# A counting sort whose one-hots and counts change their layout, and a feed-forward cut to the real nodes

## The chip, the cores and the metric

The kernel runs on one core of one Trainium2 chip, as one launch. The metric is the device time in microseconds (us). The median of the runs shown is 3781.26 us.

The engines are called as the profile calls them: PE is TensorE (PEld its weight loads), DVE is VectorE, ACT is ScalarE, POOL is GpSimd, and SP is SyncE, which issues most DMAs. Each takes its instructions in program order.

## What is computed

A graph block with three parts, over 3125 nodes of 256 features:

```python
xn = _layernorm(x)
x = x + gnn(xn, edge_attr_64, src, dst, ...)   # 103125 edges: messages, segment_sum by dst, a small MLP
      + mix(xn, ...)                           # 4 layers: linear attention with 8 heads, feed-forward 256-1024-256
x = x + moe(_layernorm(x), edge_index, ...)    # 65536 edges: graph attention gives gates, 4 experts, top 2
```

In the third part the graph attention takes its softmax and its sums over the edges that end in one node (cut to what matters):

```python
e = leaky_relu(a_src[src] + a_dst[dst])
e_max = segment_max(e, dst)
ee = exp(e - e_max[dst])
denom = segment_sum(ee, dst)
agg = segment_sum(h[src] * (ee / denom[dst])[:, :, None], dst)
```

The edges come in any order. The kernel sorts the 65536 by dst first, so that the segments become runs.

## The kernel before, in words

Nodes lie in 25 tiles of 128 rows (the last has 53 real ones), and in chunks of four tiles (seven chunks, the last with one tile).

*The order of the work.* The main program walks through the four layers of the mixing part: keys, context, attend, feed-forward up (`ff_up`, which puts a gelu of 8 blocks of 128 features into `gT`) and feed-forward down (`ff_down`). Two other streams are woven in by hand. `pace` counts estimated microseconds and emits DVE's running sums of messages (`sum_up`, tile `m_run`, L490), after each eight of which POOL gathers eight more columns (L478); once those are through, it emits POOL's sends of sorted edges (`send`, L770). `beside` emits jobs of the sort from a list: 64 count groups, `starts`, some node jobs, then 64 place groups. A scheduler then orders each engine's instructions. After the mixing part come the graph attention over the sorted edges and the four experts, with L1211, L1301 and L1312.

*The sort.* A destination has a high digit (dst // 32, 128 bins) and a low digit (dst % 32). The edges are taken 128 x 8 at a time: `GC` = 8 columns make a group, and 64 groups cover them.

- `count_group` builds a one-hot of the high digit (`oh_hi`, 128 x 8) and of the low digit (`oh_lo`, 32 x 8) on DVE (L668). Both have the column index innermost. Eight matmuls (L683) with `oh_hi[:, :, i]` stationary and `oh_lo[:, :, i]` moving give the 128 x 32 counts of each column in PSUM. ACT casts them (L685) into the f16 tile `counts`, laid as 32 low digits by 9, with slot 0 of each nine kept at zero. A DMA writes it to `counts_d`, and a matmul with the identity (L690) adds it into `table`.
- `starts` sums the table into the start of every bin.
- `place_group` reads the group's counts back as `run` (`parts`, L699) and writes into slot 0 of each nine what `split` leaves of the start after rounding (L695). DVE scans along each nine (L728), which gives running counts. ACT makes `earlier` (L741) from PE's products of the transposed high one-hot `ohT` (L740). One group later PE forms `look`: for each column a sum of matmuls with `all_h` (L746), `near`, `run` and `earlier` (L753). Each has `ohT` or `earlier` stationary, and `near`, `run[:, :, i]` or `oh_lo[:, :, i]` moving. DVE picks each edge's own entry (`own_bin`, L755) and sums it up (L756); that is the edge's place.

`near` is one contiguous row of 32 f16. `run[:, :, i]` steps by 9 elements, 18 bytes, and `oh_lo[:, :, i]` by 8 elements, 16 bytes.

*Buffers.* `run` and `oh_lo` have three buffers, `oh_hi` two, `counts` two, the PSUM tile `ps_g` two.

Of the kernel before, what the change touches and what calls it, by code (L numbers as in the profile page):

```python
# [8 lines left out]
F32 = mybir.dt.float32  # L9
BF16 = mybir.dt.bfloat16  # L10
I32 = mybir.dt.int32
F16 = mybir.dt.float16
AF = mybir.ActivationFunctionType
ALU = mybir.AluOpType
AX = mybir.AxisListType
# [3 lines left out]
P = 128  # L19
N = 3125  # L20
NT = 25
# [18 lines left out]
E2 = 65536  # L40
TE = E2 // P
NEXP = 4
GC = 8
GROUPS = TE // GC
SRC = 4096
LO = 32
# [12 lines left out]
def kernel(ctx: ExitStack, tc: tile.TileContext, a: dict, out: bass.AP):  # L59
    nc = tc.nc  # L60
    ctx.enter_context(nc.allow_non_contiguous_dma(reason="short vectors by partition"))
    V, S, G, T = nc.vector, nc.scalar, nc.gpsimd, nc.tensor

    const = ctx.enter_context(tc.tile_pool(name="const", bufs=1))
# [3 lines left out]
    pg = ctx.enter_context(tc.tile_pool(name="pg", bufs=2, space=PSUM))  # L68
    pa = ctx.enter_context(tc.tile_pool(name="pa", bufs=3, space=PSUM))
    pt = ctx.enter_context(tc.tile_pool(name="pt", bufs=2, space=PSUM))  # L70
    px = ctx.enter_context(tc.tile_pool(name="px", bufs=1, space=PSUM))
# [9 lines left out]
                    base=0, channel_multiplier=-1)  # L81
    after = const.tile([P, P], F32, name="after")
    G.affine_select(out=after, in_=ones, pattern=[[-1, P]], compare_op=ALU.is_gt, fill=0.0,
                    base=0, channel_multiplier=1)
# [13 lines left out]
    ids = const.tile([P, P], F32, name="ids")  # L98
# [81 lines left out]
    so = ctx.enter_context(tc.tile_pool(name="so", bufs=1))  # L180
# [41 lines left out]
    ps = pg.tile([P, DM], F32, name="ps_g")  # L222
# [106 lines left out]
    lo = so.tile([P, TE], F16, name="lo")  # L329
    hi = so.tile([P, TE], F16, name="hi")  # L330
# [8 lines left out]
    ps = pt.tile([P, 512], F32, name="ps_t")  # L339
# [12 lines left out]
    G.iota(bins, pattern=[[1, P], [0, GC]], base=0, channel_multiplier=0, allow_small_or_imprecise_dtypes=True)  # L352
    bin_p = const.tile([P, 1], F32, name="bin_p")
    G.iota(bin_p, pattern=[[0, 1]], base=0, channel_multiplier=1, allow_small_or_imprecise_dtypes=True)
    ident_h = const.tile([P, P], F16, name="ident_h")
    V.tensor_copy(ident_h, ident)
    all_h = const.tile([P, P], F16, name="all_h")
# [14 lines left out]
    goes = const.tile([P, LO, GC + 1], F16, name="goes")  # L372
# [9 lines left out]
    def etile(name, dt=F32, shape=(P, NT)):  # L382
        return mi.tile(list(shape), dt, name=name)

    node_n, prev_t, whole_t, above = (etile(n) for n in ("node_n", "prev_t", "whole_t", "above"))
    cnt2n = etile("cnt2n", shape=(P, 2, NT))
    sums_ps = px.tile([P, LO * GC + 2 * NT], F32, name="sums_ps")

    table, whole_ps, first_ps = sums_ps[:, :LO * GC], sums_ps[:, LO * GC:LO * GC + NT], sums_ps[:, LO * GC + NT:]

    def ends_begin():
        offs = etile("offs")
# [23 lines left out]
    cnt, own_n = etile("cnt_n"), etile("own_n")  # L416
# [249 lines left out]
    def one_hot(t, dig, n, name, bufs):  # L666
        o = so.tile([P, n, GC], F16, name=name, bufs=bufs)
        V.tensor_tensor(o, bins[:, :n, :], dig[:, t:t + GC].rearrange("p (o t) -> p o t", o=1).to_broadcast([P, n, GC]),  # L668
                        op=ALU.is_equal)
        return o  # L670

    counts_d = dram.tile([GROUPS, P, LO * (GC + 1)], F16, name="counts_d")
    counted = []
    cnts = [so.tile([P, LO, GC + 1], F16, name=f"counts{k}") for k in range(2)]
# [2 lines left out]

    def count_group(t):
        if t < TE:
            ohh, ohl = one_hot(t, hi, P, "oh_hi", 2), one_hot(t, lo, LO, "oh_lo", 3)  # L680
            ps = pg.tile([P, LO, GC], F32, name="ps_g")
            for i in range(GC):
                T.matmul(ps[:, :, i], ohh[:, :, i], ohl[:, :, i], start=i == 0, stop=i == GC - 1, skip_group_check=True)  # L683
            cnt = cnts[t // GC % 2]
            S.copy(cnt[:, :, 1:], ps)  # L685
            nc.sync.dma_start(counts_d[t // GC, :, :], cnt.rearrange("p l i -> p (l i)"))
            counted.append((t, cnt))
        if t:
            t, cnt = counted.pop(0)
            T.matmul(table, ident_h, cnt[:, :, 1:], start=t == 0, stop=t + GC == TE, skip_group_check=True)  # L690

    def split(x, near, rest):

# [1 line left out]
        V.tensor_tensor(rest[:, :, 0], x, near, op=ALU.subtract)  # L695

    def parts(t):
        cnt = so.tile([P, LO, GC + 1], F16, name="run", bufs=3)
        nc.sync.dma_start(cnt.rearrange("p l i -> p (l i)"), counts_d[t // GC, :, :])  # L699
        return (so.tile([P, LO], F16, name="near", bufs=3), cnt)  # L700

    def starts():
        cnt2 = so.tile([P, LO], F32, name="cnt2", tag="base")
        V.tensor_reduce(cnt2, table.rearrange("p (l i) -> p l i", i=GC), AX.X, ALU.add)
        cum2 = so.tile([P, LO], F32, name="cum2", tag="oh_lo", bufs=3)
        V.tensor_tensor_scan(cum2, ones[:, :LO], cnt2, 0.0, op0=ALU.mult, op1=ALU.add)
        ps = pg.tile([P, LO], F32, name="ps_g")
        T.matmul(ps[:, :1], before, cum2[:, LO - 1:], start=True, stop=True)
        V.tensor_tensor(cum2, cum2, cnt2, op=ALU.subtract)
        base2 = so.tile([P, 1], F32, name="base2")  # L710
        V.tensor_copy(base2, ps[:, :1])
        V.tensor_scalar(cum2, cum2, base2, None, op0=ALU.add)
        nc.sync.dma_start(start_d, cum2)
        V.tensor_scalar(cum2, cum2, half, None, op0=ALU.add)
        places.append(parts(0))
        split(cum2, *places[0])

    def place_group(t):

        late = looks.pop() if looks else None  # L720
        if t < TE:
            hr = so.tile([P, GC, P], F16, name="hr", bufs=2)
            nc.sync.dma_start(hr.rearrange("p t e -> p (t e)"), row_h[t // GC:t // GC + 1, :].to_broadcast([P, P * GC]))
            ohT = ohTs[t // GC % 2]
            V.tensor_scalar(ohT[:P - 1], hr[:P - 1], bin_p[:P - 1], 2.0, op0=ALU.is_equal, op1=ALU.mult)
            ohl = one_hot(t, lo, LO, "oh_lo", 3)
            near, run = places.pop()
            V.tensor_tensor_scan(run.rearrange("p l i -> p (l i)"), goes.rearrange("p l i -> p (l i)"),  # L728
                                 run.rearrange("p l i -> p (l i)"), 0.0, op0=ALU.mult, op1=ALU.add)
            if t + GC < TE:  # L730
                base = so.tile([P, LO], F32, name="base")
                V.tensor_tensor(base, run[:, :, GC], near, op=ALU.add)
                places.append(parts(t + GC))
                split(base, *places[0])

            earlier = so.tile([P, GC, P], F16, name="earlier", bufs=2)
            for i0 in range(0, GC, 4):
                ps = pt.tile([P, 4, P], F32, name="ps_t")
                for i in range(4):
                    T.matmul(ps[:, i, :], ohT[:, i0 + i, :], ohT[:, i0 + i, :], start=i == 0, stop=i == 3, skip_group_check=True)  # L740
                S.activation(earlier[:, i0:i0 + 4, :], ps, AF.Sign, bias=slope[:, 2:3], scale=slope[:, 1:2])  # L741
            looks.append((t, ohT, ohl, near, run, earlier))
        if late:
            t, ohT, ohl, near, run, earlier = late
            look = pg.tile([P, GC, LO], F32, name="ps_g")
            T.matmul(look.rearrange("p i l -> p l i"), all_h, ohl, start=True, stop=False, skip_group_check=True)  # L746
            for k in range(3):
                for i in range(GC):
                    if k == 2:
                        a1, a2 = earlier[:, i, :], ohl[:, :, i]  # L750
                    else:
                        a1, a2 = ohT[:P - 1, i, :], run[:P - 1, :, i] if k else near[:P - 1]
                    T.matmul(look[:, i, :], a1, a2, start=False, stop=k == 2, skip_group_check=True)  # L753
            own = so.tile([P, GC, LO], F32, name="own_bin", bufs=1)
            V.scalar_tensor_tensor(own, look, float(E2), ohl.rearrange("p l i -> p i l"), op0=ALU.add, op1=ALU.mult)  # L755
            V.tensor_reduce(number[t // SG % 2][:, t % SG:t % SG + GC], own, AX.X, ALU.add)  # L756
            if (t + GC) % SG == 0:
                V.tensor_scalar_mul(number[t // SG % 2], number[t // SG % 2], 0.5)
                laid(place[:, t + GC - SG:t + GC], number[t // SG % 2])
                clock["placed"] = t + GC  # L760

    places = []
# [331 lines left out]
            pace(1.9 * k / 2)  # L1094

    def ff_up(l, c, h2, f0, f1):
        w = len(c) * P
        for f in range(f0, f1):
            ps = pa.tile([P, 512], F32, name="ps_a")
            for kc in range(2):  # L1100
                T.matmul(ps[:, :w], ff_w[l]["w1"][:, kc, f * P:(f + 1) * P], h2[:, kc, :w], start=kc == 0, stop=kc == 1)  # L1101
            S.activation(gT[:, f, :w], ps[:, :w], AF.Gelu, bias=ff_w[l]["b1"][:, f:f + 1])  # L1102
            pace(1.8 * len(c) / 4)
# [267 lines left out]
    goes, whole, whole_r, ends_in = (at_end[:, i:i + 1] for i in range(2 * H4 + NCH + 2, 2 * H4 + NCH + 6))  # L1371
# [31 lines left out]
    for t0 in (0, NT // 2 + 1):  # L1403
        t1 = min(t0 + NT // 2 + 1, NT)
        ps = pa.tile([P, NT // 2 + 1, NCA], F32, name="ps_a")
# [14 lines left out]
    own = node(H4, "own")  # L1420
# [94 lines left out]
    for j, c in enumerate(PAIRS):  # L1515
        if c[0] % HALF == 0:
            gates(c[0], min(c[0] + HALF, NT))
        for i, t in enumerate(c):
            if j % 3 == 2:

                for e0 in range(0, NEXP, 2):
                    w = so.tile([P, 2, D], F32, name="weighed", tag="hr", bufs=2)
# [38 lines left out]
```

## Time and profile before

| | |
|---|---|
| median of 3 timed runs | 3781.26 us (3776.46 to 3784.04) |
| the profiled execution's own time | 3726.91 us |
| its span, first to last instruction | 3725.2 us |
| mean granted clock of TensorE | 0.762 |
| busy: PE, PEld, DVE, ACT, POOL | 2232.7, 1505.7, 1452.2, 1062.2, 1776.0 us |
| first to last column gathered (L478) | some 17 to 1640 us |
| count groups (oh_hi at L668) | mostly 201 to 435 us |
| place groups (scans at L728) | 439 to 2700 us |

A line of a group gives the source line, the engine, the operation, output and inputs by the program's names, the shape and the number; then the busy time in us and the mean ns of one, then the engine's idle time just before them and what ended it. Durations of one instruction overlap with the next one's, so on PE the distance from start to start is what an instruction takes from the engine. "remote" is a wait whose end the trace ties to no instruction; "issue" is time without a visible wait.

### The profile page before, as it was taken

The numbers are of one execution on the slowest core, as the hardware profiler recorded it, in microseconds if no ns is written. First come the engines' busy times: TensorE is split into PE (matmuls) and PEld (weight loads), VectorE is DVE, ScalarE is ACT, GpSimd is POOL, SyncE is SP. The second block draws the span as 40 slices with busy tenths as digits, with TensorE's granted clock in tenths as the row PEclk, the third lists the DMA queues.
The fourth block names the chain that finished last, engine by engine and source line by source line (L and its number), as shares of the span: only waits on it lengthen the run. The fifth ranks groups of instructions, "written<-read, shape, count | busy, mean of one in ns | idle before, by whom it ended". The sixth has DMA issues, their size and how long they took to land. (4 is left out here: it accounts for less than half of the span.)

```text
span 3725.2 us, 31745 instructions
## 1 busy us (share of the span) xinstructions
PE 2232.7 (60%) x9891; PEld 1505.7 (40%) x9891; DVE 1452.2 (39%) x4484; ACT 1062.2 (29%) x1933; POOL 1776.0 (48%) x1843
## 2 busy tenths in 40 slices
PE   3667654675667676645575466547667275747470
PEld 2545433443444455433343344435445143424250
DVE  6656544644544455532232233324422021111127
ACT  4422242233233233322232224213333021212122
POOL 2545454544445544644435434453442736464623
PEclk8878776776778887877787777768788677868685
DMA  6656564746645556722010002101100101010101
GB/s 206 193 188 201 162 199 136 211 157 192 212 150 190 176 166 209 225 80 77 20 33 18 23 18 58 43 25 35 44 10 8 16 17 30 15 29 14 27 12 36
DMA packets 300669, 359.57 MB, mean 97 GB/s; under 512 B 180576, under 2 KB 248039, under 8 KB 287687
## 3 DMA queue, kind: packets, MB, share of 16 engines
q1 hardware_dynamic: 229782, 242.00, 20.4%
q0 software_dynamic: 70704, 115.42, 11.9%
q8 instruction: 80, 1.31, 0.1%
q14 instruction: 103, 0.84, 0.1%
HBM read 201.91 MB, written 155.35 MB: 96 GB/s over the span
## 5 line engine op out<-in xcount | busy, mean ns | idle before, releaser
L478 POOL DMA_INDIRECT m_run<-xn_d,src_i x806 | 797.5, 989 | 835.9 <-issue 228.2
L770 POOL DMA_INDIRECT by_dst<-pairs,place x512 | 494.8, 966 | 280.3 <-issue 185.5
L1211 POOL DMA_INDIRECT rows_c<-tab_d,si x400 | 380.6, 952 | 301.5 <-DVE rows_c L1269 182.6
L1101 PE MATMUL ps_a<-h,w 128*128 128x512 f32 (+1 forms) x896 | 413.0, 604 | 101.5 <-ACT gT L1102 38.5
L490 DVE SCALAR_TENSOR_TENSOR m_run<-m_run,stay 128x320 f32<-128x320 f32 x805 | 437.3, 543 | 32.3 <-DMA m_run<-xn_d,src_i 17.7
L1112 PE MATMUL ps_a<-w,gT 128*128 128x256 f32 x1600 | 382.3, 394 | 20.4 <-issue 19.9
L1112 PEld LDWEIGHTS ps_a<-w,gT 128*128 128x128 f32 x1600 | 314.4, 198 | 124.2 <-issue 78.4
L1301 PE MATMUL ps_a<-hT,we 128*128 128x512 f32 (+1 forms) x448 | 226.5, 640 | 137.9 <-issue 115.1
L1101 PEld LDWEIGHTS ps_a<-h,w 128*128 128x128 f32 x896 | 173.8, 214 | 267.5 <-issue 189.5
L1312 PE MATMUL ps_t<-we,hf 128*128 128x256 f32 x800 | 203.7, 406 | 111.6 <-issue 79.1
L609 PE MATMUL ps_a<-gh,gw 128*128 128x256 f32 (+1 forms) x312 | 106.4, 489 | 207.7 <-DVE gh L612 95.8
L1312 PEld LDWEIGHTS ps_t<-we,hf 128*128 128x128 f32 x800 | 160.2, 204 | 158.5 <-issue 97.9
L1301 PEld LDWEIGHTS ps_a<-hT,we 128*128 128x128 f32 x448 | 89.7, 213 | 294.0 <-issue 259.2
L1102 ACT ACTIVATE gT<-ps_a,b 128x512 f32<-128x512 f32 (+1 forms) x224 | 141.3, 641 | 214.3 <-PE ps_a L1101 118.8
L1261 DVE COPY rows_c<-ev 128x104 f32<-128x104 f32 (+1 forms) x16 | 4.6, 286 | 481.7 <-ACT ev L1223 471.3
L559 POOL DMA_INDIRECT aggr<-run_d,sum_i x25 | 24.4, 977 | 336.2 <-PE ps_t L585 312.9
L609 PEld LDWEIGHTS ps_a<-gh,gw 128*128 128x128 f32 x312 | 72.7, 250 | 235.9 <-DVE gh L612 102.2
L741 ACT ACTIVATE earlier<-ps_t,slope 128x512 f16<-128x512 f32 x128 | 93.8, 773 | 260.0 <-PE ps_t L740 146.2
L1039 PE MATMUL ps_g<-xm,kr 128*128 128x256 f32 x400 | 127.5, 463 | 63.8 <-ACT kr L1037 36.1
L123 ACT ACTIVATE hn<-xm,rstd 128x256 f32<-128x256 f32 x225 | 121.4, 592 | 86.5 <-DVE rstd L119 57.7
L1039 PEld LDWEIGHTS ps_g<-xm,kr 128*128 128x128 f32 x400 | 88.4, 232 | 118.3 <-ACT kr L1037 58.5
L159 PE MATMUL ps_t<-ident,hn 128*128 128x128 f32 x450 | 82.7, 319 | 87.6 <-issue 37.7
(399 smaller groups left out, 3615.6 us busy)
## 6 DMA issues: line engine op xcount, KB each, us to landing
run_d<-m_run SPq DMA_DIRECT2D x100, 1280.0 KB
m_run<-in_edge_attr_dram SPq DMA_DIRECT2D x95, 256.0 KB
hr<-row_h SPq DMA_DIRECT2D x64, 256.0 KB
m_run<-xn_d,src_i POOLq DMA_INDIRECT x806
w<-in_L_mix_W_dram SPq DMA_DIRECT2D x8, 1024.0 KB
by_dst<-pairs,place POOLq DMA_INDIRECT x512
rows_c<-tab_d,si POOLq DMA_INDIRECT x400
run_d<-rows_c SPq DMA_DIRECT2D x15, 312.0 KB
```

The source lines that it names most:

```text
L123: S.activation(dst, src, AF.Identity, bias=r[:, 1, i:i + 1], scale=r[:, 0, i:i + 1])
L478: last_gather[0] = G.indirect_dma_start(out=m[:, t, :D], out_offset=None, in_=xn_d, in_offset=bass.IndirectOffsetOnAxis(ap=src_i[:, t0 + t ...
L490: add = V.scalar_tensor_tensor(m[:, t, :], before_m, stay[:, c:c + 1], m[:, t, :], op0=ALU.mult, op1=ALU.add)
L609: T.matmul(ps[:, :w], gw[i][:, kc, m * P:(m + 1) * P], h[:, kc, :w], start=kc == 0, stop=kc == 1)
L770: i = G.indirect_dma_start(out=by_dst, out_offset=bass.IndirectOffsetOnAxis(ap=place[:, t:t + 1], axis=0), in_=pairs0[:, t:t + 1], in_offs ...
L1039: T.matmul(ps_x[:, m, :], kr[:, m * P:(m + 1) * P], xm[:, t, :], start=i == 0 and m == 0, stop=i == len(c) - 1, skip_group_check=True)
L1101: T.matmul(ps[:, :w], ff_w[l]["w1"][:, kc, f * P:(f + 1) * P], h2[:, kc, :w], start=kc == 0, stop=kc == 1)
L1102: S.activation(gT[:, f, :w], ps[:, :w], AF.Gelu, bias=ff_w[l]["b1"][:, f:f + 1])
L1112: T.matmul(ps[:, i, :], gT[:, f, (2 * i0 + i) * P:(2 * i0 + i + 1) * P], ff_w[l]["w2"][:, f, :], start=False, stop=f == FF // P - 1, skip_ ...
L1211: G.indirect_dma_start(out=rows_c[:, t - COLS[j], :], out_offset=None, in_=tab_d, in_offset=bass.IndirectOffsetOnAxis(ap=si[:, t:t + 1], a ...
L1301: T.matmul(ps[:, :w], we1[:, kc, f * P:(f + 1) * P], hT[:, kc, c[0] * P:c[0] * P + w], start=kc == 0, stop=kc == 1)
L1312: T.matmul(ps[:, i, :], hh[f][:, (i0 + i) * P:(i0 + i + 1) * P], we2[:, f, :], start=False, stop=f == FF2 // P - 1, skip_group_check=True)
```

## The change

The low one-hot gets the column index outside and the low digit inside (`low_hots`), compared with a new f16 ramp `low_ids`. The counts in PSUM have the same layout, and ACT's cast turns them back to 32 by 9 while it writes. The matmul into the table takes all nine slots, zeros included, and the table is 288 wide. After the scan a new ACT copy `run_c` turns the eight running counts of each digit into a contiguous row for each column; it takes the buffers of `counts`, and `run` has two buffers in place of three. `ff_up` takes only the 53 real nodes of the last chunk.

```diff
+    low_ids = const.tile([P, LO], F16, name="low_ids")
+    V.tensor_copy(low_ids, ids[:, :LO])
...
+    TW = LO * (GC + 1)
+    sums_ps = px.tile([P, TW + 2 * NT], F32, name="sums_ps")
...
+    def low_hots(t):
+        o = so.tile([P, GC, LO], F16, name="oh_lo", bufs=3)
+        V.tensor_tensor(o, low_ids.rearrange("p (o l) -> p o l", o=1).to_broadcast([P, GC, LO]),
+                        lo[:, t:t + GC].rearrange("p (t o) -> p t o", o=1).to_broadcast([P, GC, LO]), op=ALU.is_equal)
+        return o
...
-            ohh, ohl = one_hot(t, hi, P, "oh_hi", 2), one_hot(t, lo, LO, "oh_lo", 3)
-            ps = pg.tile([P, LO, GC], F32, name="ps_g")
+            ohh, ohl = one_hot(t, hi, P, "oh_hi", 2), low_hots(t)
+            ps = pg.tile([P, GC, LO], F32, name="ps_g")
             for i in range(GC):
-                T.matmul(ps[:, :, i], ohh[:, :, i], ohl[:, :, i], start=i == 0, stop=i == GC - 1, skip_group_check=True)
+                T.matmul(ps[:, i, :], ohh[:, :, i], ohl[:, i, :], start=i == 0, stop=i == GC - 1, skip_group_check=True)
             cnt = cnts[t // GC % 2]
-            S.copy(cnt[:, :, 1:], ps)
+            S.copy(cnt[:, :, 1:].rearrange("p l i -> p i l"), ps)
...
-            T.matmul(table, ident_h, cnt[:, :, 1:], start=t == 0, stop=t + GC == TE, skip_group_check=True)
+            T.matmul(table, ident_h, cnt.rearrange("p l i -> p (l i)"), start=t == 0, stop=t + GC == TE, skip_group_check=True)
...
-        cnt = so.tile([P, LO, GC + 1], F16, name="run", bufs=3)
+        cnt = so.tile([P, LO, GC + 1], F16, name="run", bufs=2)
...
-            ohl = one_hot(t, lo, LO, "oh_lo", 3)
-            near, run = places.pop()
-            V.tensor_tensor_scan(run.rearrange("p l i -> p (l i)"), goes.rearrange("p l i -> p (l i)"),
-                                 run.rearrange("p l i -> p (l i)"), 0.0, op0=ALU.mult, op1=ALU.add)
+            ohl = low_hots(t)
+            near, run_l = places.pop()
+            V.tensor_tensor_scan(run_l.rearrange("p l i -> p (l i)"), goes.rearrange("p l i -> p (l i)"),
+                                 run_l.rearrange("p l i -> p (l i)"), 0.0, op0=ALU.mult, op1=ALU.add)
+            run = so.tile([P, GC, LO], F16, name="run_c", tag=f"counts{t // GC % 2}")
+            S.copy(run, run_l[:, :, :GC].rearrange("p l i -> p i l"))
...
-            T.matmul(look.rearrange("p i l -> p l i"), all_h, ohl, start=True, stop=False, skip_group_check=True)
+            T.matmul(look, all_h, ohl, start=True, stop=False, skip_group_check=True)
...
-                        a1, a2 = earlier[:, i, :], ohl[:, :, i]
+                        a1, a2 = earlier[:, i, :], ohl[:, i, :]
...
-                        a1, a2 = ohT[:P - 1, i, :], run[:P - 1, :, i] if k else near[:P - 1]
+                        a1, a2 = ohT[:P - 1, i, :], run[:P - 1, i, :] if k else near[:P - 1]
...
-            V.scalar_tensor_tensor(own, look, float(E2), ohl.rearrange("p l i -> p i l"), op0=ALU.add, op1=ALU.mult)
+            V.scalar_tensor_tensor(own, look, float(E2), ohl, op0=ALU.add, op1=ALU.mult)
...
     def ff_up(l, c, h2, f0, f1):
-        w = len(c) * P
+        w = min((c[-1] + 1) * P, N) - c[0] * P
```

More of the change, by code (lines that the diff above doesn't have):

```diff
@@ L386 @@
     cnt2n = etile("cnt2n", shape=(P, 2, NT))
-    sums_ps = px.tile([P, LO * GC + 2 * NT], F32, name="sums_ps")
-    table, whole_ps, first_ps = sums_ps[:, :LO * GC], sums_ps[:, LO * GC:LO * GC + NT], sums_ps[:, LO * GC + NT:]
+    TW = LO * (GC + 1)
+    sums_ps = px.tile([P, TW + 2 * NT], F32, name="sums_ps")
+    table, whole_ps, first_ps = sums_ps[:, :TW], sums_ps[:, TW:TW + NT], sums_ps[:, TW + NT:]
     def ends_begin():
@@ L703, in starts @@
         cnt2 = so.tile([P, LO], F32, name="cnt2", tag="base")
-        V.tensor_reduce(cnt2, table.rearrange("p (l i) -> p l i", i=GC), AX.X, ALU.add)
+        V.tensor_reduce(cnt2, table.rearrange("p (l i) -> p l i", i=GC + 1), AX.X, ALU.add)
         cum2 = so.tile([P, LO], F32, name="cum2", tag="oh_lo", bufs=3)
@@ L725, in place_group @@
             V.tensor_scalar(ohT[:P - 1], hr[:P - 1], bin_p[:P - 1], 2.0, op0=ALU.is_equal, op1=ALU.mult)
-            ohl = one_hot(t, lo, LO, "oh_lo", 3)
-            near, run = places.pop()
-            V.tensor_tensor_scan(run.rearrange("p l i -> p (l i)"), goes.rearrange("p l i -> p (l i)"),
-                                 run.rearrange("p l i -> p (l i)"), 0.0, op0=ALU.mult, op1=ALU.add)
+            ohl = low_hots(t)
[4 more added lines that the diff above has]
+            S.copy(run, run_l[:, :, :GC].rearrange("p l i -> p i l"))
             if t + GC < TE:
                 base = so.tile([P, LO], F32, name="base")
-                V.tensor_tensor(base, run[:, :, GC], near, op=ALU.add)
+                V.tensor_tensor(base, run_l[:, :, GC], near, op=ALU.add)
                 places.append(parts(t + GC))
```

## The prediction

> **What bounds the kernel now.** I read the page's busy shares and slices first. No engine is full: TensorE (PE) leads with 60%, its granted clock swings around 0.76, and GpSimd (POOL), which issues the gathers and the sends, has 48%. The chain of waits follows only the last few per cent back, so it can't name the bound of the stages in which the sort runs.
>
> ```profile
> span 3725.2 us, 31745 instructions
> PE 2232.7 (60%) x9891; PEld 1505.7 (40%) x9891; DVE 1452.2 (39%) x4484; ACT 1062.2 (29%) x1933; POOL 1776.0 (48%) x1843
> ...
> PE   3667654675667676645575466547667275747470
> ```
>
> So I take PE's in-order stream as what carries the time, with holes: in the timeline I found 68 holes of over 5 us between matmuls, 911 us together, most with POOL alone at work. POOL's gathers (L478) wait 184.9 us for VectorE's (DVE) m_run sums, and those hardly wait for a gather: they follow the program's order, so the gathers don't lead. Next, the groups by line and shape, where the sort is seen:
>
> ```profile
> L753 PE MATMUL ps_g<-oh_lo,earlier 128*128 128x32 f16 x512 | 47.5, 236 | 25.7 <-issue 24.1 <-ACT earlier L741 1.5
> L753 PE MATMUL ps_g<-run,ohT 127*128 127x32 f16 x512 | 45.7, 237 | 16.4 <-issue 15.4 <-DVE run L728 0.8
> L683 PE MATMUL ps_g<-oh_lo,oh_hi 128*128 128x32 f16 x512 | 42.9, 243 | 2.6 <-DVE oh_hi L668 1.3 <-DVE oh_lo L668 1.2
> L755 DVE SCALAR_TENSOR_TENSOR own_bin<-ps_g,oh_lo 128x256 f32<-128x256 f32 x64 | 38.2, 596 | 244.2 <-remote 198.0 <-PE ps_a L1101 23.1 <-PE ps_a L1090 12.5
> L668 DVE TENSOR_TENSOR oh_lo<-bins,lo 128x256 f16<-128x256 f16 x128 | 35.6, 281 | 0.0
> L753 PE MATMUL ps_g<-near,ohT 127*128 127x32 f16 x512 | 30.6, 187 | 9.2 <-issue 9.0
> L685 ACT CAST counts<-ps_g 128x256 f16<-128x256 f32 x64 | 22.7, 372 | 92.3 <-issue 33.2 <-PE ps_g L683 25.6 <-DMA counts_d<-counts 22.4
> L594 DVE SCALAR_TENSOR_TENSOR h<-ps_a,xr 128x256 f32<-128x256 f32 x25 | 10.5, 420 | 47.0 <-PE ps_a L593 35.0 <-remote 6.9 <-PE ps_a L1101 4.6
> L633 DVE TENSOR_TENSOR h<-h,go 128x256 f32<-128x256 f32 x25 | 10.4, 418 | 10.4 <-ACT h L123 10.4
> ```
>
> The reader should see that three matmul groups of one shape differ: near (contiguous) 187 ns, run and oh_lo (a step of 18 and of 16 bytes) 237. These overlap, so the price is the distance from start to start. PE's timeline gives it:
>
> ```profile
> 1490.78 0.38 PE L746 MATMUL ps_g<-oh_lo,all_h 128*128 128x256 f16 x1
> 1490.95 0.40 PE L753 MATMUL ps_g<-near,ohT 127*128 127x32 f16 x8
> 1491.20 0.65 PE L753 MATMUL ps_g<-run,ohT 127*128 127x32 f16 x8
> 1491.67 0.67 PE L1090 MATMUL ps_a<-co,hT 128*128 128x256 f32 x2
> ```
>
> Eight near take 1491.20 - 1490.95 = 0.25 us, eight run 0.47. Over the whole trace the middle distance is 25 ns for near, 60 for run, oh_lo and 63 for L683.
>
> [...] L755 with its strided oh_lo takes 596 ns, L594, the same operation on PSUM without a strided source, 420.
>
> **The change part by part.**
>
> *Look matmuls (L753).* 1024 of them (run and earlier) go from about 59 to 25 ns: 34 x 1024 = 35 us of PE; by the rows of eight above (0.22 us x 128) 28. What follows them in the trace decides what counts: 526 stand in batches after which the next matmul starts within 0.3 us (18 us, counted whole), 372 before a hole of 0.3 to 2 us (13 us, half: 6), 126 before longer holes (4 us, none). Sum 24 us; bounds 12 and 35.
>
> *Look's first matmul (L746)* gets a contiguous PSUM output. Start to next start is 0.17 us now; the plain 256-wide L690 has 0.12: 0.05 x 64 = 3 us, half on the path: 1.5.
>
> *Count matmuls (L683).* The moving operand becomes contiguous, the stationary ohh[:, :, i] stays strided; its weight loads last 160 ns against 111 at L753. The trace has no such pair: at worst 63 stays (0 us), at best 25 (512 x 38 = 19 us). I take 50, since the slower load probably holds: 6.6 us, and half, 3, because the counts also wait for ACT and for counts_d (22.4 us at L685).
>
> *L690* becomes 288 wide and contiguous: 0.12 us now, an estimate of the same. Zero: the 32 columns more stand against the steps less, up to 1 us either way.
>
> *Feed-forward.* 128 matmuls of the last chunk shrink to 53 columns. The keys' own 53-wide matmuls (L981) have the same middle distance as the 128-wide ones of L1101, 112 ns, so PE gains nothing; the 32 gelus shrink from 367 ns by an estimated 62 (75 elements at 0.83 ns, the slope between 128x512 at 686 and 128x128 at 367 being similar). 2 us, of which 1 counts: PE bounds that chunk.
>
> *New ACT copy run_c,* 64 of 256 elements from an 18-byte step. Nearest row: L685, 372 ns; [...] A strided read could add the 0.18 us that DVE shows: 0.58. I take 0.40: 26 us busy (37 at 0.58). It waits for the scan L728, and behind it on ACT stand earlier (L741), gelus, hn and kr, for which PE waits. I laid the copies, in the changed program's ACT order, over the trace of before: in 49 of 64 places the scan is done and ACT then idles at least 0.45 us, which hides the copy. 15 have no such room: 6 us. In some ten dense groups the run matmuls also wait 1 to 2.5 us for the copy that now stands between them and the scan, mostly where DVE has no idle anyway: 3 us. If the cover of the 49 is gone, 20 us more.
>
> *DVE.* low_hots reads lo with an inner step of 0. [...] L633's 418 ns in place of 281, 128 x 137 = +17.5 us (bounds 0 and 20). L755 reads oh_lo contiguous: 596 to L594's 420, 64 x 176 = -11 (bounds -13 and 0). Sum +6; DVE is 39% busy, but full in the dense groups: 3 us.
>
> *L685* now writes at an 18-byte step: 0 to 0.18 x 64 = 11 us on ACT; I take 0, as ACT waits for counts_d there.
>
> *Queues.* SP has the same 64 counts_d writes and 64 run reads, each within some fifteen places of where it was; POOL's order is the same. With two run buffers in place of three a read waits for the copy and the base sum of the group before, not for the look two groups back; both end within a few us of each other: 0, up to 5 us if the read is late, since L695 already waits 49.8 us for such reads. run_c takes the count tiles, free once the counting is over.
>
> Sum: 24 + 1.5 + 3 + 1 = 29.5 gained, 6 + 3 + 3 = 12 lost: 17.5 us less. Against the profiled execution's own 3726.9 (span 3725.2) that is 3709. The timed runs' median, 3781.3, is 54 us longer than the profiled one; I carry the difference over: **3764**.
>
> **The rivals.** *Hidden:* the holes set the time, and a shorter burst makes the next hole longer. For it: 911 us of holes. Against it: half the strided matmuls are followed at once. PE's relief and the extra work cancel: 3781. *Slower:* the copy makes ACT the bound. It puts an in-order engine between DVE and PE; at 0.58 us with none hidden it costs 37 us, DVE 6, against 24 + 1.5 gained (L683 staying at 63): 3781 + 18 = 3799. It decides from 29.5 / 64 = 0.46 us per group on the path. For it: ACT is what PE waits for before L740 and L1101. Against it: ACT's 29% and the 49 places. *All passes:* PE's stream is the time; 35 + 3 + 10 gained, little lost: 3735. That L683 doesn't become faster at all, so that the change does only half of what it says, costs the likeliest case 3 us.
>
> **The numbers.** 3764 has 0.55 (own range 3750 to 3773), hidden 0.14, slower 0.22, all passes 0.09. A measurement of this kernel tells about 0.2% (7.6 us) from no change. Faster 0.64, same 0.14, slower 0.22. The range, 3730 to 3798, takes in most of the slower case and nearly all of the fastest.
>
> **What would show it.** L753 from start to start: 25 ns for all three kinds; L746 0.12; L683 40 to 60; oh_lo on DVE near 418 ns and L755 near 420; 64 run_c near 0.40 us. Idle time of ACT before run_c named by the scan, or of PE at L753 by run_c, of over 20 us would speak for the slower case. The prediction is wrong if run and oh_lo keep 60 ns, or if PE's busy time falls by 40 us and the span doesn't.

## The result and the profile after

| | before | after |
|---|---|---|
| median of four timed runs, us | 3778.86 (3770.96 to 3784.04) | 3735.76 (3727.97 to 3746.08) |
| ratio, 95% interval | | 0.9889 [0.9858, 0.9920] |
| profiled execution, its own time (span), us | 3726.91 (3725.2) | 3746.08 (3744.4) |

The changed kernel is faster, by 43 us in these runs. Two further comparisons of the same two kernels, on other occasions, gave 0.9935 and 0.9909 (below); the three together say about 0.991, or 34 us. The forecast was 17.5 us.

The two spans point the other way: the profiled execution of after is 19 us longer than that of before. Neither is wrong. One execution is one draw: other profiled executions had a span of 3736.7 us for before, and of 3755.0 and 3713.8 us for after, on other occasions (the timed median of before itself lay between 3714 and 3779 us on them). With such a scatter a difference of 1% can't be read from two spans. What a trace does tell is the duration of each row, which repeats within a few per cent (the cast L694: 1399, 1390 and 1394 ns in the three profiles of after), so the page is read for rows and the timed runs for the sum.

The head of the page of after, busy time of each engine:

```profile
span 3744.4 us, 31831 instructions
...
PE 2214.7 (59%) x9891; PEld 1484.7 (40%) x9891; DVE 1458.1 (39%) x4485; ACT 1151.1 (31%) x1996; POOL 1778.0 (47%) x1843
```

PE is busy 18 us less than in the profile of before (2232.7; another profile of before has 2246.5), DVE 6 more (1452.2), as forecast, ACT 89 more (1062.2 before). The gain came although ACT's added work is far more than what left PE. The groups by line and shape of after (busy us, mean ns of one, idle time before them and what ended it) answer to those shown of before; L753 became L764, L683 L692, L685 L694, L755 L766, L668 L677 (for oh_lo), L746 L757:

```profile
L694 ACT CAST counts<-ps_g 128x256 f16<-128x256 f32 x64 | 80.0, 1399 | 65.4 <-remote 30.3 <-PE ps_g L692 23.3 <-DMA counts_d<-counts 7.4
L677 DVE TENSOR_TENSOR oh_lo<-low_ids,lo 128x256 f16<-128x256 f16 x128 | 52.8, 415 | 0.0
L740 ACT COPY run_c<-run 128x256 f16<-128x256 f16 x64 | 41.8, 657 | 108.8 <-remote 77.5 <-PE ps_g L764 11.0 <-issue 9.9
L692 PE MATMUL ps_g<-oh_lo,oh_hi 128*128 128x32 f16 x512 | 40.8, 216 | 3.4 <-issue 3.4
L764 PE MATMUL ps_g<-oh_lo,earlier 128*128 128x32 f16 x512 | 29.5, 179 | 24.4 <-issue 22.5 <-ACT earlier L752 1.6
L764 PE MATMUL ps_g<-near,ohT 127*128 127x32 f16 x512 | 29.2, 180 | 31.0 <-issue 30.9
L766 DVE SCALAR_TENSOR_TENSOR own_bin<-ps_g,oh_lo 128x256 f32<-128x256 f32 x64 | 26.7, 417 | 257.8 <-remote 187.3 <-PE ps_a L1112 34.3 <-issue 19.1
L764 PE MATMUL ps_g<-run_c,ohT 127*128 127x32 f16 x512 | 26.3, 180 | 38.7 <-issue 23.8 <-ACT run_c L740 9.9 <-ACT earlier L752 4.9
L1113 ACT ACTIVATE gT<-ps_a,b 128x53 f32<-128x53 f32 x32 | 9.1, 309 | 10.9 <-PE ps_a L1112 5.5 <-remote 2.5 <-PE ps_t L1046 1.8
```

Three things are to be seen. The three kinds of look matmul now agree (179 to 180 ns; before 187, 237, 236). The cast of the counts went from 372 to 1399 ns, and the new copy run_c takes 657: these two make 99 us (57 and 42), more than ACT's whole increase of 89. And oh_lo went from 281 to 415 ns on DVE, while own_bin fell from 596 to 417.

Mean durations of matmuls overlap, so their price is read from start to start in the timeline of PE in after (start us, duration us, group, idle before it and its releaser):

```profile
1505.15 0.27 PE L757 MATMUL ps_g<-oh_lo,all_h 128*128 128x256 f16 x1
1505.26 0.36 PE L764 MATMUL ps_g<-near,ohT 127*128 127x32 f16 x8
1505.46 0.35 PE L764 MATMUL ps_g<-run_c,ohT 127*128 127x32 f16 x8
...
1508.71 0.35 PE L764 MATMUL ps_g<-run_c,ohT 127*128 127x32 f16 x8 [0.47 <-issue]
1508.91 0.35 PE L764 MATMUL ps_g<-oh_lo,earlier 128*128 128x32 f16 x8
...
1521.90 0.38 PE L764 MATMUL ps_g<-run_c,ohT 127*128 127x32 f16 x8 [0.80 <-ACT run_c L740]
```

Eight run_c matmuls take 1508.91 - 1508.71 = 0.20 us, where eight run matmuls took 0.47; L757 is followed after 0.11 us, not 0.17. Over the whole trace the middle distance is 25 ns for near, run_c and oh_lo, and 109 ns after L757. The last line above is one of the few places where PE waits for the new copy.

For the count matmuls the middle distance is 62 ns in after and 62 to 63 in before: their mean duration fell from 243 to 216 ns, their price did not. Eight of them in the timeline of before, and the start of what follows:

```profile
263.24 0.67 PE L683 MATMUL ps_g<-oh_lo,oh_hi 128*128 128x32 f16 x8
263.72 0.40 PE L1109 MATMUL ps_a<-b_parts,ones_b 65*128 65x512 bf16 x1
```

Eight of them in after, 0.49 us where it was 0.48:

```profile
278.82 0.66 PE L692 MATMUL ps_g<-oh_lo,oh_hi 128*128 128x32 f16 x8
279.31 0.59 PE L1120 MATMUL ps_a<-b_parts,ones_b 65*128 65x512 bf16 x1
```

The waits of after (us in total, times, longest):

```profile
ACT run_c L740 <- remote: 77.5, 8, 32.0
...
PE ps_g L764 <- issue: 77.2, 67, 3.7
...
PE sums_ps L699 <- ACT counts L694: 32.2, 29, 8.6
...
DVE run L704 <- DMA run<-counts_d: 24.9, 7, 15.8
...
PE ps_g L764 <- ACT run_c L740: 9.9, 4, 5.6
```

PE waits 9.9 us for run_c, four times. This wait differs from profile to profile. In the second profile of after it is:

```profile
PE ps_g L764 <- ACT run_c L740: 35.7, 6, 16.1
```

In the third it is 3.8 us, and in the three profiles of other kernels below that have the copy 3.9 to 14.7. So the copy does sit on PE's path at times. The wait of DVE for the reads of counts_d didn't grow with one run buffer less: 24.9 us here, 11 to 25 in all six profiles with two buffers, 27 to 50 in the eight with three. "Issue" ahead of the look matmuls (idle time in which PE waits for nothing that the profile shows) rose from the 48.5 us of before's look rows to 77.2.

### The profile page after: what moved, and what is told of

It is laid out like the page before. It is cut to its first block, busy times and chain, and to the rows that moved or that the text cites. A ratio compares the mean times of both kernels' runs of the same rounds, so it can differ in the third digit from the quotient of the medians.

```text
span 3744.4 us, 31831 instructions
## 1 busy us (share of the span) xinstructions
PE 2214.7 (59%) x9891; PEld 1484.7 (40%) x9891; DVE 1458.1 (39%) x4485; ACT 1151.1 (31%) x1996; POOL 1778.0 (47%) x1843
## 5 line engine op out<-in xcount | busy, mean ns | idle before, releaser
L1112 PE MATMUL ps_a<-h,w 128*128 128x512 f32 (+1 forms) x896 | 417.4, 610 | 89.3 <-ACT h L164 56.6
L1112 PEld LDWEIGHTS ps_a<-h,w 128*128 128x128 f32 x896 | 175.0, 216 | 256.1 <-issue 178.6
L1024 PE MATMUL ps_a<-wq,h 128*128 128x256 f32 x400 | 115.9, 427 | 45.2 <-issue 25.6
```

## The experiments

The expectations name theories by a letter. **M**: PE's relief in the look matmuls carries the gain. **H**: the holes in PE's stream take it up, so that less PE work doesn't show. **S**: ACT's strided copies cost as much as the contiguous matmuls bring. **C**: the new layout of the counting brings the gain. **F**: the feed-forward cut does. **N**: the measured difference is mostly chance. Ratios are to the kernel before, in five rounds on the same chip; 0.1% is 3.7 us. A ratio isn't exactly the quotient of the two medians given beside it (3744.13 / 3773.61 would be 0.9922).

One thing holds for every edit below but that of the cast: it also changes the order in which the scheduler puts the instructions. Against the order of before, at least 46 of PE's 9891 matmuls stand elsewhere with the feed-forward cut alone, 91 with the placing alone, 122 with the counting alone, 265 in the changed kernel, and 345 in the kernel with more matmuls, the added ones left out. (Counted in the traces, whose order on PE is the same in all profiles of one kernel. In the trace of before it is that of the program too: where matmuls of one source line are taken as one, all 1497 stretches stand in it as compiled. So do, counted alike, all 871 on ACT, 45 on POOL and 505 of the DMAs that SP issues, and 3414 of 3416 on DVE.) What a new order is worth by itself, no run measures.

### The same two kernels again

The changed kernel, unedited:

> The changed kernel once more, with more rounds, beside the kernel before on the same chip. Theory M (TensorE's relief in the look matmuls carries the gain): ratio 0.985 to 0.993 again, L764 25 ns from start to start, L694 near 1400 ns. Theory N (the gain is a matter of how the holes of one pair of programs happen to fall on one chip): the ratio moves by over 0.5% from 0.989.

Measured: 0.9935 [0.9904, 0.9965], 3744.13 against 3773.61 us. A third time, on another occasion:

> The changed kernel a third time, as the neighbour of the next three on one chip. Theory M: 0.9935 within 0.003, by the sum of the place groups' 0.994 and little else.

Measured: 0.9909 [0.9873, 0.9945], 3730.03 against 3764.12 us. And the kernel before against itself:

> The kernel before against itself, a control for how far equal programs differ here. Both theories: 1.000, within 0.0025. If it comes out at 0.997, the 0.997 of the feed-forward cut alone and of the count groups alone is what any program gets against the kernel before, and tells nothing of those parts.

Measured: 1.0003 [0.9978, 1.0028]. So N falls as chance of the measurement: the gain is there in all three comparisons, none of whose intervals reaches 1. But one comparison is uncertain by 0.2 to 0.5%, 7 to 17 us, which is as much as single parts of the change bring. And the control is the same program in the same order, so it doesn't tell what a new order of the instructions can bring. The first ratio, 0.9889, was on the good side.

### The three parts, each alone

Feed-forward alone, twice:

```diff
-        w = len(c) * P
+        w = min((c[-1] + 1) * P, N) - c[0] * P
```

> The kernel before with only the feed-forward cut to the 53 real nodes of the last chunk. Theory M: 1 to 2 us less, no difference that can be told (0.999 to 1.000), since TensorE's matmuls of that chunk stay at 112 ns from start to start. Rival F (a stage of each layer waits for the last chunk): 5 us or more less, 0.9985 or lower.

> The kernel before with only the feed-forward cut, a second time. If the 0.9971 of the first time was chance: 0.9985 or higher, as 32 gelus shortened by 62 ns are worth 2 us. If the cut has an effect that the trace doesn't show: 0.9971 within 0.0025 again.

Measured: 0.9971 [0.9949, 0.9994] and 0.9980 [0.9961, 1.0000].

The placing alone: low_hots in the look, run_c, contiguous operands and output of the look matmuls, two run buffers; the counting as before:

```diff
-            ohl = one_hot(t, lo, LO, "oh_lo", 3)
-            near, run = places.pop()
+            ohl = low_hots(t)
+            near, run_l = places.pop()
...
+            run = so.tile([P, GC, LO], F16, name="run_c", tag=f"counts{t // GC % 2}")
+            S.copy(run, run_l[:, :, :GC].rearrange("p l i -> p i l"))
...
-                        a1, a2 = earlier[:, i, :], ohl[:, :, i]
+                        a1, a2 = earlier[:, i, :], ohl[:, i, :]
```

> The kernel before with the place groups alone changed: low_hots, run_c, contiguous look matmuls, two run buffers; count groups and feed-forward as before. Theory M: it holds the whole gain and more, since the counts cost time: 40 to 70 us less (0.982 to 0.990). Rival C (the counts' and the table's layout brings the gain): under 15 us less (0.996 or higher).

Measured: 0.9940 [0.9916, 0.9963], 23 us (14 to 32) less. Its groups show that the place part alone has the short look matmuls and the cheap cast:

```profile
L740 ACT COPY run_c<-run 128x256 f16<-128x256 f16 x64 | 41.8, 656 | 110.8 <-remote 80.8 <-PE ps_g L764 12.2 <-issue 9.0
...
L764 PE MATMUL ps_g<-run_c,ohT 127*128 127x32 f16 x512 | 27.5, 180 | 33.9 <-issue 26.1 <-ACT run_c L740 5.7 <-ACT earlier L752 2.1
...
L694 ACT CAST counts<-ps_g 128x256 f16<-128x256 f32 x64 | 22.7, 372 | 111.7 <-remote 36.9 <-PE ps_g L692 35.2 <-issue 24.2
```

The counting alone: low_hots in the counting, ps_g and the cast, the 288 wide table; the placing as before:

```diff
-            ps = pg.tile([P, LO, GC], F32, name="ps_g")
+            ps = pg.tile([P, GC, LO], F32, name="ps_g")
...
-                T.matmul(ps[:, :, i], ohh[:, :, i], ohl[:, :, i], start=i == 0, stop=i == GC - 1, skip_group_check=True)
+                T.matmul(ps[:, i, :], ohh[:, :, i], ohl[:, i, :], start=i == 0, stop=i == GC - 1, skip_group_check=True)
...
-            S.copy(cnt[:, :, 1:], ps)
+            S.copy(cnt[:, :, 1:].rearrange("p l i -> p i l"), ps)
```

> The kernel before with the count groups and the table alone changed; place groups and feed-forward as before. Theory M: slower or the same, 0 to 40 us more (1.000 to 1.010), because the cast L694 grows from 372 to 1399 ns, 66 us of ScalarE over 64 groups, while the matmuls stay at 60 ns from start to start. Rival C: 30 us or more less (0.992 or lower).

Measured: 0.9967 [0.9942, 0.9992], 12 us (3 to 22) less, with the cast at 1409 ns and the count matmuls 62 ns apart.

The parts add up: 0.60 + 0.33 + 0.25% (mean of the two feed-forward runs) = 1.2%, against 0.9% for the whole, within their errors. The expectations were not met as they were written: M had 40 to 70 us for the placing alone and none or a loss for the counting, C had 30 us or more for the counting, and F's 5 us or more are reached by both middle values, not by the whole of both intervals. The placing has the largest part, as M says, the counting and the feed-forward smaller ones, and each part's share is known to some 10 us only. As each edit comes with a new order, these are the shares of edit and order together.

### The cast, in the cheap direction

The PSUM tile keeps its new layout, but ACT walks it so that the writes to cnt are in order and the reads from PSUM take the step:

```diff
-            S.copy(cnt[:, :, 1:].rearrange("p l i -> p i l"), ps)
+            S.copy(cnt[:, :, 1:], ps.rearrange("p i l -> p l i"))
```

In the whole changed kernel, twice:

> The changed kernel, with the cast L694 walking the digits outside and the columns inside, so that ScalarE writes runs of eight and reads PSUM at a step of 128 bytes. If the short writes at 18 bytes make the 1399 ns: the cast falls to 370 to 500 ns, ScalarE's busy time by some 60 us, and, if the cast holds up the count stage, the time falls by 10 to 40 us against the changed kernel (0.983 to 0.991 of the kernel before). If the transposition costs on either side: it stays over 1000 ns and the ratio at 0.993.

> The changed kernel with the cheap cast (374 ns), a second time, beside the changed kernel on the same chip. If ScalarE's 66 us in the count stage are on the path by a third or more: at least 20 us faster than the changed kernel (0.005 lower). If they lie beside other work: less than 8 us (under 0.002 lower).

Measured: 0.9914 [0.9874, 0.9955], and 0.9867 [0.9821, 0.9913] on the chip on which the changed kernel had 0.9909 (3721.04 against 3730.03 us). The group of the first of these:

```profile
L694 ACT CAST counts<-ps_g 128x256 f16<-128x256 f32 x64 | 22.6, 374 | 98.7 <-remote 32.7 <-PE ps_g L692 31.2 <-DMA counts_d<-counts 16.2
```

The same elements in the other order take 374 ns in place of 1399. That takes 57 us off ACT, and PE's order of instructions is the same. The time falls by 9 us in the medians where the two ran side by side (16 by the ratios), with overlapping intervals; the other ratio, 0.9914, is no lower than the changed kernel's 0.9911 in the mean. Where the rest went is seen in the stretch of the counting, from its third oh_hi (two are made early) to its last (start:end, us, then busy us of PE, its loads, DVE, ACT, POOL with counts, the granted clock, DMA share, GB/s). The changed kernel, in its third comparison:

```profile
207.20:441.70 234.50, 151.72 (x888) 108.39 (x888) 139.75 (x317) 117.08 (x130) 117.57 (x114) 0.74 0.57 181
```

With the cheap cast, on the same chip:

```profile
206.30:432.50 226.20, 152.33 (x891) 107.15 (x890) 138.14 (x317) 64.78 (x130) 119.05 (x114) 0.75 0.59 188
```

ACT is busy 117 us against 65 in this stretch, which is only 8 us longer: most of the costly cast lies in time in which ACT would have idled. With the counting alone the stretch is even shorter with the costly cast (222.1 us) than with the cheap one (229.5). The version with the cheap cast isn't shown apart from the changed kernel.

The counting alone with the cheap cast (the edit of the counting above, with this cast):

> The kernel before with the count groups and the table alone changed, with the cheap cast. TensorE's count matmuls keep 60 ns, VectorE has 64 x 135 ns = 9 us more, ScalarE nothing. If the 0.9967 of the count groups alone was chance: 1.000 within 0.0025. If the new layout of the counts does shorten the count stage: 0.997 or lower.

Measured: 0.9935 [0.9905, 0.9966], 24 us (13 to 36) less; its interval overlaps that with the costly cast (0.9967). So the kernels with the new counting are faster in both cases, though its matmuls are no faster. The same stretch in the kernel before (its second profile) shows what else changed:

```profile
202.10:436.50 234.40, 156.12 (x917) 107.94 (x918) 130.53 (x319) 65.24 (x133) 116.65 (x114) 0.79 0.57 182
```

It holds 917 matmuls there against 888 and 891. Counted in PE's order, from the first to the last count matmul, all five kernels with the old counting (before twice, placing alone, feed-forward alone, more matmuls) have 96 feed-forward matmuls (L1101) in between, and all eight with the new one have 80. The edit of the counting moved 16 of them behind the last group, some 16 x 0.47 = 7.5 us of PE by the row's 417.4 us for 896 (L1112 in after). This is of the size by which the stretch is shorter, 232.4 against 240.5 us from count matmul to count matmul in the mean of these kernels, which scatter from 218 to 241 and from 233 to 249. It is work moved, not saved. What the timed 12 to 24 us of the counting part consist of stays open: the new order, the PSUM writes that are now contiguous, or the table's plain read. No run separates these.

### Without the copy run_c

The changed kernel, but the run matmuls read the scanned tile with its 18-byte step, and run has three buffers as before:

```diff
-            run = so.tile([P, GC, LO], F16, name="run_c", tag=f"counts{t // GC % 2}")
-            S.copy(run, run_l[:, :, :GC].rearrange("p l i -> p i l"))
+            run = run_l
...
-                        a1, a2 = ohT[:P - 1, i, :], run[:P - 1, i, :] if k else near[:P - 1]
+                        a1, a2 = ohT[:P - 1, i, :], run[:P - 1, :, i] if k else near[:P - 1]
```

> The changed kernel without the copy run_c: the 512 run matmuls read the scan's tile at 18 bytes again (three buffers), all else as changed. TensorE has 512 x 35 ns = 18 us more, ScalarE 42 us less. Theory M: half of TensorE's 18 us comes back, while the copy's own cost on the path goes; 0 to 10 us more than the changed kernel (0.9935 to 0.996). Rival S (the copy costs as much as it brings): the same as the changed kernel or faster by up to 15 us (0.989 to 0.9935).

Measured: 0.9976 [0.9943, 1.0009]. The group:

```profile
L763 PE MATMUL ps_g<-run,ohT 127*128 127x32 f16 x512 | 46.3, 237 | 22.1 <-issue 17.8 <-DVE run L737 4.2
```

The run matmuls are back at 237 ns. Most of the gain is gone: 0.24% is left of the 0.9% that the changed kernel has in the mean of its three comparisons (0.9911, uncertain by 0.19%). The difference, 0.65%, is 24 us, with the errors of both 10 to 38, from different occasions. M had 10 us at most. S, that the copy costs as much as it brings, falls: with the copy, for 42 us of ACT's time, the kernel is faster. How much of the 24 us is the copy's and how much the order's (64 matmuls stand elsewhere) isn't shown; the run matmuls' own distances are 512 x 36 ns = 18 us.

### More work on PE at the same place

The kernel before, with an added matmul (the same stationary operand, a moving operand of zeros) ahead of each near and run matmul, 1024 in all, each with a weight load of its own:

```diff
+                    if k < 2:
+                        T.matmul(look[:, i, :], a1, goes[:a1.shape[0], :, 0], start=False, stop=False, skip_group_check=True)
```

> The kernel before with 1024 matmuls more in the look: before each matmul of near and of run one with the same weights and a moving operand of zeros at a step of 18 bytes, which adds nothing to the sum. It prices TensorE time in the place groups: 1024 x 60 ns = 61 us more of TensorE. Theory M (half to all of it passes): 30 to 61 us more (1.008 to 1.016). Rival H (the holes take it up): under 8 us more (1.002 or less).

Measured: 1.0111 [1.0075, 1.0148], 41 us (28 to 55) more. PE's busy time is 2304.7 us against 2246.5 for before on the same chip, 58 more. At first sight 0.7 of it reaches the end. The waits of PE warn against that reading. Of this kernel:

```profile
PE ps_g L755 <- issue: 120.6, 103, 3.2
...
PE ps_g L754 <- issue: 82.4, 66, 3.3
```

Of before, on the same chip:

```profile
PE ps_g L753 <- issue: 54.4, 54, 3.3
```

Idle time of PE for no reason that the profile shows grew by 120.6 + 82.4 - 54.4 = 149 us. It isn't spread evenly. Most of it lies in stretches in which PE starts one instruction at a time at multiples of 0.70 us, whatever its size. A piece of one such stretch in this kernel:

```profile
1841.79 0.22 PE L755 MATMUL ps_g<-run,ohT 127*128 127x32 f16 x1 [2.58 <-issue]
1844.58 0.22 PE L754 MATMUL ps_g<-goes,ohT 127*128 127x32 f16 x1 [2.58 <-issue]
1847.38 0.22 PE L755 MATMUL ps_g<-run,ohT 127*128 127x32 f16 x1 [2.58 <-issue]
1850.88 0.59 PE L609 MATMUL ps_a<-gh,gw 128*128 128x256 f32 x1 [3.28 <-issue]
1853.68 0.59 PE L609 MATMUL ps_a<-gh,gw 128*128 128x256 f32 x1 [2.21 <-issue]
```

The starts are 2.79, 2.80, 3.50 and 2.80 us apart, and the last two matmuls are large ones of another part. Counted over a trace, where at least five starts in a row lie so, these stretches make 221 us in each of the two profiles of before and 348 us here; the sum of before lies between 190 and 223 us, as the match is taken tighter or looser. What brings PE into them no run shows. So 41 us at the end stand against 58 us of work and 149 us of such gaps. The run shows that more work on PE at this place is not simply swallowed by the holes, so H as the only rule (1.002 or less) falls; it gives no share.

The same wait tells what became of part of the relief. Ahead of the look matmuls it is 48.5, 54.4, 70.4, 66.8 and 64.0 us in five profiles with the old look (before twice, feed-forward alone the second time, the counting alone with either cast), 60.8 in the mean. With the new look (after three times, placing alone, cheap cast twice) it is 77.2, 77.1, 57.5, 79.8, 82.5 and 75.5, mean 74.9. The two sets overlap, but their means differ by 14 us, some 6 either way by their scatter: about that much of what the faster matmuls saved seems to have come back in the same rows as idle time. The 0.70 us stretches hold most of it (36 of the 48.5 us in before, 62 of the 77.2 in after).

## Why the prediction was right or wrong

**Look matmuls: right.** 25 ns for all three kinds, as forecast, 1024 x 35 = 36 us of PE. It counted 24 of 35. The placing alone saved 23 us (14 to 32), where the forecast's terms for it make some 17 (24 + 1.5, less 9 for run_c, DVE about even). The two agree, but the interval is too wide to tell whether a third of the relief is lost, and the 23 us include whatever the new order does. Part of the loss seems to have taken another way than the one laid out: some 14 us came back as idle time in the look rows, which the batches counted beforehand couldn't show. That run and oh_lo would come down to near's 25 ns was the forecast's estimate, and they did; no two matmuls of either trace start less than 24 ns apart.

**L746: right,** from 174 ns among the closest and 192 in the middle of its 64 to 109 (L757), 4 to 5 us where 3 were taken. **L690: right,** nothing to be seen: where the next start follows within 0.3 us it comes after 158 ns in the mean before and 160 after.

**Count matmuls (L683): wrong.** I took 50 ns; 62 remained, the bad end of the bounds. With a strided stationary operand (loads of 162 ns at L692, 98 to 99 at L764) a contiguous moving one brings nothing that can be seen. That the stationary operand's step is what holds them is my guess: no run makes that operand contiguous.

**The counting as a whole: the term that was mis-sized most for the time.** Its terms came to about zero (3 for L683, nothing for the cast, some for DVE's longer oh_lo against it); alone it measured 12 and, with the cheap cast, 24 us less. The gain comes from something that is no term of my sum, and its cause stays open. The one thing seen is that the edit moved PE's order, at least 122 matmuls in all, 16 feed-forward ones out of the counting. I had compared the order of ACT, SP and POOL, and not asked what of other work a re-planned PE would carry inside the stretch.

**L685 on ACT: wrong by far in size, nearly right in effect.** I took 0 with a bound of 0.18 us each, borrowed from DVE's reads; it measured 1.03 us more each (372 to 1399), 57 more on ACT in all. The effect on the time is not resolved (9 to 16 us in one comparison, nothing in the other): most of the cover I named, ACT's idle time in the counting, held.

**run_c: wrong in size, its effect about right.** 0.66 us, outside the bound of 0.58; I took 0.40. Both lie 0.03 us above what rows of before give, L685's 372 ns and that with DVE's 0.18 us on it; the rest was my estimate. A cast that writes in order stays at the row's time (374 ns where it reads PSUM at a step); the copy with a strided read of SBUF (657) and the cast with a strided write (1399) don't, so that row didn't price these two. PE waits 9.9 us for run_c in the first profile of after, where I counted 6 + 3, but that is a lucky agreement: the six profiles with the copy have 3.8 to 35.7 us. The 35.7 are over the 20 us that I had named as a sign of the slower case; that profile has a long span (3755.0 us), yet the kernel as timed beside it was faster than before (0.9935).

**DVE: right.** oh_lo 415 ns (418 forecast from L633), own_bin 417 (420). The rows L633 and L594 priced both. The new oh_lo reads each element of lo 32 times in a row, and at the same 256 elements it takes 415 ns in place of 281; low_ids took the place of bins in the same edit, and no run parts the two. At own_bin the f16 step of 16 bytes had cost (596 - 417) / 256 = 0.70 ns an element.

**Queues: right that they cost nothing.** DVE's wait for the reads of counts_d didn't grow with one run buffer less (11 to 25 us against 27 to 50).

**Feed-forward: right in the rows** (gelu 367 to 309 ns, 58 against the forecast 62, which was 75 elements at the slope (686 - 367) / 384 = 0.83 ns of before's own gelu rows; the middle distance of PE's matmuls stays 112 ns). The timed 8 and 11 us are more than the 1 counted, but the intervals reach down to 0 and 2 us, and this edit too moves at least 46 matmuls in PE's order.

**The rivals.** *Slower*: ACT became 89 us busier, the copy cost more than the price from which that rival was worked out (0.66 against 0.58 us), and the kernel is faster all the same; the cover of ACT's idle time decided, not the price. *Hidden*: as the only rule it is refuted by the gain, and by the added matmuls; that the holes take up a part isn't refuted. *All passes* gave 3735, the very number of the first measurement, but not for its reason: its 10 us from the count matmuls don't exist, the look's relief doesn't pass whole, and the rest comes from the counting part. A number that fits is no proof of its mechanism. The likeliest case's own range, 3750 to 3773, was missed: by the first measurement clearly, by the mean of the three (0.9911 of 3781 is 3748) narrowly.

In sum, of the 17.5 us the look's part (about 17) was sound in its distances and measured 23 with the placing alone; the missing 15 to 25 us are those of the counting, 12 to 24, with a few from the feed-forward. Whether these come from the edits themselves or from the new order of instructions stays open.

## What to carry to other kernels

Give a matmul with few columns a contiguous moving operand (with 32 columns, 25 ns from start to start in the look in place of 60), and let an engine with idle time at that place make the layout, even for more busy time than it saves (42 us of ACT for 18 us of PE); but price a matmul by the distance of starts (the count matmuls' mean duration fell from 243 to 216 ns, their distance only from 63 to 62), and look whether the stationary operand is strided too (it is in these, and the contiguous moving operand brought nothing). When ACT must transpose from PSUM, let it read with a step and write SBUF in order (374 ns where the strided write took 1399). Before a part is called worth nothing, compare the order of the busiest engine in both programs, and measure each part alone. A control of equal kernels shows the noise of the measurement (1.0003 here); it doesn't show what a new order of instructions does, and a small edit brings one (at least 46 matmuls with the feed-forward cut).

## What the runs showed of the hardware that was not expected

- ACT, 256 elements a partition: writing f16 at an 18-byte step takes 1399 ns, writing in order 374, the source being the same PSUM tile: (1399 - 374) / 256 = 4.0 ns an element. Reading f16 at an 18-byte step takes 657. Reading f32 from PSUM at a 128-byte step, with writes in order, costs nothing to be seen (374 against 372 for a plain read).
- Matmuls with 32 columns are 60 to 63 ns apart with a strided moving operand (16 or 18 bytes), 25 with a contiguous one, and still 62 with a contiguous one in the counting, where the stationary operand is strided.
- A 256 wide matmul with a permuted PSUM output (L746) is followed after some 174 ns at the closest and 192 in the middle, with a plain one (L757) after 109 in the middle.
- PE has stretches in which it starts one instruction at a time at multiples of 0.70 us, small and large matmuls alike: 221 us in both profiles of before, 348 with 1024 more small matmuls. With the added matmuls came 149 us of idle time with no releaser in the trace, beside 58 us of work. The cause isn't shown.
